# Graph attention on one core: one hold a block for the row gathers, query and key reflected per head, one merged product, and the first gathers spread over the first stage

## The chip, the cores and the metric

The kernel runs on one core of one Trainium2 chip. The core has five engines, each with a queue of its own: TensorE (PE: matrix products and transposes into PSUM; PEld is its weight load), VectorE (DVE), ScalarE (ACT), GpSimd (POOL) and SyncE (SP). [...] The metric is the device time of one execution in microseconds (us). Lower is better.

## The reference

A graph of 12,500 nodes and 212,500 edges, 128 features, eight heads of 16. The edges are sorted by their destination.

```python
h = jnp.maximum(_layernorm(x, axis=-1), 0.0)
q = (h @ Wq.T + bq).reshape(N, 8, 16)
k = (edge_attr @ Wk.T + bk).reshape(-1, 8, 16)
v = (h @ Wv.T + bv).reshape(N, 8, 16)
qs, qd = q[src], q[dst]
in_m   = jnp.sum(qs * k,  axis=-1)
out_m  = jnp.sum(qd * k,  axis=-1)
diag_m = jnp.sum(qs * qd, axis=-1)
score = (_segment_softmax(in_m / 4, dst, N) + _segment_softmax(out_m / 4, dst, N)
         + _segment_softmax(diag_m / 4, dst, N)) * edge_weight ** lam
h = segment_sum(score[..., None] * v[dst], dst)
return x + leaky_relu(h.reshape(N, 128) @ Wo.T + bo, 0.1)
```

Three logits for each edge and head, each a sum over 16 features; for these, only inner products of q and k within a head matter, so any rotation or reflection applied to both within a head leaves them as they are.

## The kernel before

**First stage.** 25 groups of four tiles of 128 nodes. In turn g, from -2 on, ACT rectifies group g+2 (`rectify`, L932), PE turns group g+1 (`turn_h`, L939; ACT copies it to hT, L941) and projects group g to q (`nodes_q`, L947); DVE adds the bias (L950) and SP stores the rows into `q_table` in DRAM. Beside it, DVE takes the statistics of the layer norm (L1064), and `aside(turn)` does other small jobs of that turn.

**Gathers.** For each edge the row of its source node is fetched by an indirect DMA on POOL (`gather`, L706): a block is 512 edges, four gathers of 128 rows of 128 floats. The first `RAW` = 24 blocks fetch rows of x and compute q from them in the loop, so they need not wait for q_table: 15 blocks are issued in turn -2 and 9 in turn 9 of the first stage. Five more blocks, and some single rows, fetch from q_table once it is whole.

**Main loop.** 415 blocks, one an iteration g; five blocks (s = g mod 5) are a turn t. In iteration g

- POOL gathers the rows of block g+26 (`LOOK`), into one of 28 buffers;
- PE turns the edge features of block g+2 (`turn`, tile eT_ps with one buffer, L1247; ACT copies them out, L1249), spreads q to the edges of block g+1 by a one-hot product (`spread_q`, qd_ps, L1264; ACT copies it to qd, L1267) and computes k of block g+1 (`project`: the bias as a product of 3 rows and 512 columns, L1254, then four products with the weights, L1256);
- DVE forms the three products of block g and sums them by head (`logits`, L1275 to L1278);
- ACT makes the one-hot rows of block g+3 (L697, L698).

By s, other steps on a whole turn follow: scans along the edges for the maxima and sums (L1338 to L1390), the exponentials, the selection of the ends of segments (`show_ends`, d_ps L1423, then ACT's L1426 and L1427), and the rows of sums (w_ps L1437, l_ps L1298).

**Order.** `pin` ties each instruction behind the previous one on its engine, so every engine works in the order in which the code is written. A dictionary `behind` holds POOL back: gather j of block g+26 waits, by a semaphore, for a PE instruction of iteration g-1.

```python
if (g - LOOK, j) in behind:
    tc.add_manual_dep(rows.ins, behind[g - LOOK, j], ...Sync..., reason="close behind the products")
```

`behind[g+1, 0]` is the last transpose of `turn(g + 2)`, `[g+1, 1]` the last product of `spread_q(g + 1)`, `[g+1, 2]` that of `project(g + 1)`, and `[g+1, 3]` PE's last instruction of the steps by s.

Of the kernel before, what the change touches and what calls it, by code (L numbers as in the profile page):

```python
# [7 lines left out]
F32 = mybir.dt.float32  # L8
# [8 lines left out]
HEADS = 8  # L17
DIM = 16
# [454 lines left out]
def ordered_path(ctx: ExitStack, tc: tile.TileContext, flag, x, src, dst, edge_attr, edge_weight,  # L473
# [102 lines left out]

    eps = consts.tile([P, 1], F32, name="eps")
# [17 lines left out]
    bv3, bk3, bo3 = [b3[:, i, None, :].to_broadcast([3, JN, F]) for i in range(3)]  # L595
    bq_all = consts.tile([P, F], F32, name="bq_all")
# [105 lines left out]
    def gather(g):  # L702
        if g < end:
            qq = qqs[g] = firsts[g] if g < FIRST else gath.tile([P, JN, F], F32, name="qq")
            for j in range(JN):
                rows = pin(nc.gpsimd.indirect_dma_start(  # L706
                    out=qq[:, j, :], out_offset=None, in_=x if g < RAW else q_table,
                    in_offset=bass.IndirectOffsetOnAxis(
                        ap=sources[g // S][:, g % S, j:j + 1], axis=0)))
# [63 lines left out]
    with tc.tile_pool(name="prep", bufs=1) as prep, \  # L773
# [4 lines left out]
        lam_sb = prep.tile([RW, 1], F32, name="lam_sb")  # L778
        w_in = prep.tile([P, 4, F], F32, name="w_in")
# [24 lines left out]
        pin(nc.sync.dma_start(bq_all, bq[None, :].to_broadcast([P, F])))  # L804
# [10 lines left out]
        def load_b():  # L815
            for i, b in enumerate((bv, bk, bo)):
                pin(nc.sync.dma_start(b_row[:, i, :], b[None, :]))

# [85 lines left out]

        def turn_w(i, to):
# [143 lines left out]
        turn_w(0, wq)  # L1049
# [189 lines left out]
    with tc.tile_pool(name="work", bufs=2) as work, \  # L1239
            tc.tile_pool(name="scan", bufs=2) as scan, \  # L1240
            tc.tile_pool(name="ps", bufs=1, space=PSUM) as ps:
        ks, eTs, qds, q_ps, lTs = {}, {}, {}, {}, {}
# [9 lines left out]
        def project(g):  # L1252
            k_ps = ks[g] = ps.tile([P, JN, F], F32, name="k_ps", bufs=2)
            pin(nc.tensor.matmul(k_ps, ones3, bk3, start=True, stop=False))  # L1254
            for j in range(JN):
                pin(nc.tensor.matmul(k_ps[:, j, :], eTs[g][:, j, :], wk, start=False,  # L1256
                                     stop=(j == JN - 1)))
            del eTs[g]

        def spread_q(g):  # L1260
            s, d = g % S, st[g // S]
            qd_ps = q_ps[g] = ps.tile([P, JN, F], F32, name="qd_ps", bufs=2)
            for j in range(JN):
                pin(nc.tensor.matmul(qd_ps[:, j, :], ohs[g][:, j * P:(j + 1) * P],  # L1264
                                     d["win"][:, s, :], start=(j == 0), stop=(j == JN - 1)))
            qds[g] = work.tile([P, JN, F], F32, name="qd")
            pin(nc.scalar.copy(qds[g], qd_ps))  # L1267
            del ohs[g]

        def logits(g):  # L1270
# [4 lines left out]
            pin(nc.vector.tensor_mul(prod[:, :, 1, :], qqs[g], q_ps[g]))  # L1275
            pin(nc.vector.tensor_mul(prod[:, :, 0, :], qqs[g], ks[g]))  # L1276
            pin(nc.vector.tensor_mul(prod[:, :, 2, :], qds[g], ks[g]))  # L1277
# [3 lines left out]
            del ks[g], qds[g], q_ps[g], qqs[g]  # L1281
# [397 lines left out]
        turn(0)  # L1679
        spread_q(0)  # L1680
        project(0)
        turn(1)
        raw_rectify(SOON)
        for g in range(end):
# [7 lines left out]
            if g + 2 < end:  # L1692
                turn(g + 2)
                behind[g + 1, 0] = pinned[products]
            if g + 1 < end:
                spread_q(g + 1)
# [39 lines left out]
            behind[g + 1, 3] = pinned[products]  # L1736
# [63 lines left out]
        names = ("eT_ps", "k_ps", "qd_ps", "qd_ps", "k_ps")  # L1800
        for r in range(len(rest) + 2):
            if r < len(rest):
                of = rest[r]
                of.score = score[:, r * JN:(r + 1) * JN]
                scores_of(ends_ab[:, r * JN:r * JN + of.n], of.score[:, :of.n])
                of.weigh(of.held)
                of.turn(small([P, JN, P], "node_ps"))
                of.project_o(ps.tile([P, JN, F], F32, name=names[r], bufs=1 if r == 0 else 2))
# [48 lines left out]
```

## Time and profile before

| | |
|---|---|
| median of 3 runs (lowest to highest) | 2730.74 us (2729.23 to 2732.47) |
| the profiled execution: its own time, its span | 2727.95 us, 2726.2 us |
| mean granted clock of TensorE (1 is full) | 0.745 |
| busy: PE, DVE, ACT, POOL | 71%, 76%, 52%, 58% |
| gathers from q_table (L706): count, busy, mean | 1564, 1479.2 us, 946 ns |
| L706, idle before it | 912.7 us, 336.7 of it "issue" |
| first stage / loop with gathers / rest, from the timeline | to about 205 us / to 2543 us / to 2726 us |

A group of instructions reads: line, engine, operation, destination <- sources, shapes, count, then busy time and the mean of one in ns, then the time that the engine stood idle just before them and what ended it. "remote" is a releaser which the profile can't name; "issue" is time in which the engine waited for nothing that is seen. A row of waits gives the engine, its line, the releaser, and after the colon the sum in us, how often, and the longest. A row of the timeline gives the start and the duration in us.

### The profile page before, as it was taken

How to read it: one execution, taken by the hardware profiler on the slowest of the kernel's cores; microseconds unless marked ns; L12 is line 12 of the kernel's file. 1: busy time of each engine (PE TensorE's matmuls, PEld its weight loads, DVE VectorE, ACT ScalarE, POOL GpSimd, SP SyncE). 2: the span in 40 equal slices, each digit the busy share in tenths (PEclk: the TensorE clock that was granted, in tenths of full speed). 3: DMA queues.
4: the chain of work that ended last, by engine and by line, in shares of the span. 5: the costliest groups of instructions: out<-in, count | busy, mean ns of one | idle time of the engine just before them, and what ended most of it. 6: DMA issues, size and time to landing. Idle time of an engine off the chain costs nothing.

```text
span 2726.2 us, 37924 instructions
## 1 busy us (share of the span) xinstructions
PE 1941.1 (71%) x10956; PEld 1524.3 (56%) x10956; DVE 2071.3 (76%) x2887; ACT 1409.7 (52%) x2662; POOL 1585.3 (58%) x1683
## 2 busy tenths in 40 slices
PE   2366776777767777677777777777777776777885
PEld 1245655555555555555555655656556565555664
DVE  2265887777778778778877878877878787787995
ACT  1355864445555555555545555554545555555673
POOL 7516566666666666666666666666666666666200
PEclk9876887776777777777667767766767677776786
DMA  6256444544454454544445444444444544454431
GB/s 177 76 165 175 133 123 126 141 140 127 132 146 132 134 147 140 138 138 125 140 121 137 131 128 132 131 130 123 128 141 112 140 135 121 128 139 129 125 85 52
DMA packets 378950, 355.75 MB, mean 130 GB/s; under 512 B 192898, under 2 KB 298637, under 8 KB 378527
## 3 DMA queue, kind: packets, MB, share of 16 engines
q1 hardware_dynamic: 310109, 238.12, 30.6%
q0 software_dynamic: 53184, 108.92, 15.1%
q10 hardware_dynamic: 15440, 6.20, 0.9%
q8 instruction: 90, 1.47, 0.2%
q14 instruction: 127, 1.04, 0.1%
HBM read 320.83 MB, written 32.17 MB: 129 GB/s over the span
## 4 chain that ended last, share of the span: by engine, by line
PE 44%; DVE 16%; ACT 13%; another core or an unknown queue 12%; issue 11%; DMA 1%; DVEq 1%; POOL 1%; SPq 0%; ACTq 0%; POOLq 0%
PE k_ps L1256 12%; PE w_ps L1437 7%; PE eT_ps L1247 7%; DVE lT L1278 4%; PE qd_ps L1264 4%; PE k_ps L1254 3%; PE node_ps L1186 2%; DVE prod L1276 2%; ACT qd L1267 2%; ACT relb L697 2%; DVE prod L1275 2%; DVE prod L1277 2%; ACT oh L698 2%; PE m_ps L1381 2%
## 5 line engine op out<-in xcount | busy, mean ns | idle before, releaser
L706 POOL DMA_INDIRECT qq<-q_table,sources x1564 | 1479.2, 946 | 912.7 <-issue 336.7
L1278 DVE TENSOR_REDUCE lT<-prod 128x96 f32<-128x1536 f32 x415 | 727.4, 1753 | 14.3
L1256 PE MATMUL k_ps<-wk,eT 128*128 128x128 f32 x3320 | 621.5, 343 | 18.8 <-issue 17.1
L1256 PEld LDWEIGHTS k_ps<-wk,eT 128*128 128x128 f32 x3320 | 524.3, 240 | 171.6 <-issue 170.6
L1247 PE MATMUL eT_ps<-ident,ea 128*128 128x128 f32 x1660 | 346.5, 345 | 206.6 <-issue 129.7
L1276 DVE TENSOR_TENSOR prod<-qq,k_ps 128x512 f32<-128x512 f32 x412 | 280.7, 681 | 203.5 <-remote 166.3
L1247 PEld LDWEIGHTS eT_ps<-ident,ea 128*128 128x128 f32 x1660 | 247.9, 178 | 286.2 <-issue 173.1
L1249 ACT COPY eT<-eT_ps 128x512 f32<-128x512 f32 x415 | 240.7, 580 | 322.8 <-remote 122.6
L1267 ACT COPY qd<-qd_ps 128x512 f32<-128x512 f32 x415 | 244.8, 590 | 313.1 <-PE qd_ps L1264 88.5
L1437 PE MATMUL w_ps<-back,sel 128*126 128x144 f32 (+1 forms) x1296 | 232.1, 356 | 169.0 <-ACT sel L1427 134.4
L1275 DVE TENSOR_TENSOR prod<-qq,qd_ps 128x512 f32<-128x512 f32 x412 | 279.9, 679 | 89.2 <-issue 47.9
L1437 PEld LDWEIGHTS w_ps<-back,sel 128*126 128x126 f32 (+1 forms) x1296 | 218.2, 247 | 183.4 <-ACT sel L1427 144.2
L697 ACT ACTIVATE relb<-relb,before 126x512 bf16<-126x512 bf16 x415 | 303.1, 730 | 0.0
L1277 DVE TENSOR_TENSOR prod<-qd,k_ps 128x512 f32<-128x512 f32 x415 | 281.8, 679 | 0.0
L698 ACT ACTIVATE oh<-relb 126x512 bf16<-126x512 bf16 x415 | 261.3, 630 | 13.2
L1264 PE MATMUL qd_ps<-win,oh 126*128 126x128 bf16 x1660 | 205.6, 258 | 26.6 <-issue 13.7
L1254 PE MATMUL k_ps<-b,ones 3*128 3x512 bf16 x415 | 191.4, 461 | 23.0 <-DVE prod L1277 10.9
L1264 PEld LDWEIGHTS <-oh 126*128 126x128 bf16 x1660 | 164.2, 120 | 48.0 <-issue 34.1
L1381 PE MATMUL m_ps<-ident,m 120*128 120x120 f32 x332 | 76.1, 364 | 107.6 <-issue 59.0
L1426 ACT ACTIVATE sel<-d_ps 128x420 f32<-128x420 f32 x168 | 78.5, 514 | 139.0 <-remote 127.7
L1391 ACT ACTIVATE back<-back 128x480 f32<-128x480 f32 x83 | 50.0, 602 | 142.6 <-DVE back L1390 63.2
L1381 PEld LDWEIGHTS m_ps<-ident,m 120*128 120x128 f32 x332 | 53.1, 215 | 124.5 <-issue 82.6
(234 smaller groups left out, 1934.9 us busy)
## 6 DMA issues: line engine op xcount, KB each, us to landing
ea<-in_edge_attr_dram SPq DMA_DIRECT2D x415, 256.0 KB
relb<-rel_d SPq DMA_DIRECT2D x83, 630.0 KB
qq<-q_table,sources POOLq DMA_INDIRECT x1564
win<-q_table SPq DMA_DIRECT2D x415, 31.5 KB
far<-far_d SPq DMA_DIRECT2D x84, 120.2 KB
q_table<-q SPq DMA_DIRECT2D x24, 384.0 KB
sums<-rows SPq DMA_DIRECT2D x411, 7.9 KB
q_table<-xq SPq DMA_DIRECT2D x24, 256.0 KB
```

The costliest lines, as they stand in the source:

```text
L697: pin(nc.scalar.activation(d, d, AF.Abs, bias=before[:K3]))
L698: pin(nc.scalar.activation(oh, d, AF.Relu, bias=1.0, scale=-1.0))
L706: rows = pin(nc.gpsimd.indirect_dma_start(out=qq[:, j, :], out_offset=None, in_=x if g < RAW else q_table, in_offset=bass.IndirectOffsetOn ...
L1247: pin(nc.tensor.transpose(eT_ps[:, j, :], eas[g][:, j * F:(j + 1) * F], ident))
L1256: pin(nc.tensor.matmul(k_ps[:, j, :], eTs[g][:, j, :], wk, start=False, stop=(j == JN - 1)))
L1264: pin(nc.tensor.matmul(qd_ps[:, j, :], ohs[g][:, j * P:(j + 1) * P], d["win"][:, s, :], start=(j == 0), stop=(j == JN - 1)))
L1267: pin(nc.scalar.copy(qds[g], qd_ps))
L1275: pin(nc.vector.tensor_mul(prod[:, :, 1, :], qqs[g], q_ps[g]))
L1276: pin(nc.vector.tensor_mul(prod[:, :, 0, :], qqs[g], ks[g]))
L1277: pin(nc.vector.tensor_mul(prod[:, :, 2, :], qds[g], ks[g]))
L1278: pin(nc.vector.tensor_reduce(lTs[t][:, :, s, :], prod.rearrange("p j i (h d) -> p j (i h) d", d=DIM), AX.X, ALU.add))
L1437: pin(nc.tensor.matmul(w_ps[:(hi - lo) * W, lo:hi].rearrange("p s c -> p (s c)"), d["sel"][:n, j, lo:hi, :].rearrange("p s w -> p (s w)"), ...
```

## The change

- **One hold a block.** `gather` of block g+26 takes one hold, on its first gather: the last product of `spread_q(g)`. The other three of a block have none.
- **q and k reflected.** Ahead of the first stage a Householder reflection per head is worked out from bk (`bring_to_size`, `reflect`: some twenty small VectorE operations and one root on ACT), which turns bk's 16 elements of a head onto the first. Wq, Wk and bq are reflected with it (the turn of the weights by the identity becomes a product with `axes`). So k's bias has one element a head, and is added by a product of 3 rows and 32 columns, now behind k's four products.
- **Merged product.** q and k of a block lie in one PSUM tile `qk_ps` (two buffers), k is projected ahead of q, and one VectorE product of 1024 elements replaces two of 512.
- **First gathers spread.** Of the 24 raw blocks six are issued in turn -2, the others one a turn in 18 of the turns 0 to 21, each with its first gather held behind the last product of that turn's `nodes_q`.

```diff
-    def gather(g):
+    def gather(g, held=None):
...
-                if (g - LOOK, j) in behind:
-                    tc.add_manual_dep(rows.ins, behind[g - LOOK, j], mybir.DependencyInfo(
+                held = behind.get((g - LOOK, j), held)
+                if held is not None:
+                    tc.add_manual_dep(rows.ins, held, mybir.DependencyInfo(
...
+                held = None
...
+        def bring_to_size():
+            pin(nc.vector.tensor_reduce(top, heads_of(bk_all), AX.X, ALU.max))
...
+            pin(nc.scalar.activation(low, square, AF.Sqrt))
...
+        def reflect():
...
+            pin(nc.vector.tensor_copy(axes, ident))
+            v_both = v[:, None, :].to_broadcast([P, 2, F])
+            pin(nc.vector.tensor_mul(w, turned, v_both))
...
+            pin(nc.vector.tensor_sub(turned, turned, w))
...
         def turn_w(i, to):
-            pin(nc.tensor.transpose(w_ps, w_in[:, i, :], ident))
+            if i in (0, 2):
+                pin(nc.tensor.matmul(w_ps, w_in[:, i, :], axes, start=True, stop=True))
...
-        turn_w(0, wq)
+        bring_to_size()
...
+            if g == -2:
+                reflect()
             if 0 <= g + 1 < GN:
                 turn_h(g + 1)
+            if g == -1:
+                turn_w(0, wq)
             if g >= 0:
                 nodes_q(g)
...
-            if g == -2:
-                for of in range(3 * S):
-                    gather(of)
+            for of in range(RAW):
+                turn = (5 * of - 30) // 4
+                if max(turn, -2) == g:
+                    gather(of, pinned[str(mybir.EngineType.PE)] if g >= 0 else None)
             aside(g)
             if g == 9:
                 fetch_few()
-                for of in range(3 * S, RAW):
-                    gather(of)
...
         def project(g):
-            k_ps = ks[g] = ps.tile([P, JN, F], F32, name="k_ps", bufs=2)
-            pin(nc.tensor.matmul(k_ps, ones3, bk3, start=True, stop=False))
+            qks[g] = ps.tile([P, 2, JN, F], F32, name="qk_ps", bufs=2)
+            k_ps = qks[g][:, 0]
             for j in range(JN):
-                pin(nc.tensor.matmul(k_ps[:, j, :], eTs[g][:, j, :], wk, start=False,
-                                     stop=(j == JN - 1)))
+                pin(nc.tensor.matmul(k_ps[:, j, :], eTs[g][:, j, :], wk, start=(j == 0), stop=False))
+            pin(nc.tensor.matmul(k_ps.rearrange("p j (h d) -> p j h d", d=DIM)[:, :, :, 0], ones3, bk_lead,
+                                 start=False, stop=True))
...
-            pin(nc.vector.tensor_mul(prod[:, :, 1, :], qqs[g], q_ps[g]))
-            pin(nc.vector.tensor_mul(prod[:, :, 0, :], qqs[g], ks[g]))
-            pin(nc.vector.tensor_mul(prod[:, :, 2, :], qds[g], ks[g]))
+            pin(nc.vector.tensor_mul(prod[:, :, 0:2, :].rearrange("p j i f -> p i j f"),
+                                     qqs[g][:, None].to_broadcast([P, 2, JN, F]), qks[g]))
+            pin(nc.vector.tensor_mul(prod[:, :, 2, :], qds[g], qks[g][:, 0]))
...
             if g + 2 < end:
                 turn(g + 2)
-                behind[g + 1, 0] = pinned[products]
             if g + 1 < end:
+                project(g + 1)
                 spread_q(g + 1)
-                behind[g + 1, 1] = pinned[products]
-                project(g + 1)
-                behind[g + 1, 2] = pinned[products]
+                behind[g + 1, 0] = pinned[products]
...
-            behind[g + 1, 3] = pinned[products]
```

On PE, one iteration of the loop before (eT_ps: the turned edge features; oh: one-hot rows; win: the window of q; b and ones: bias and ones; three more pairs of LDWEIGHTS and MATMUL on oh are left out):

```order
L1247 MATMUL eT_ps<-ident,ea 128x128 x4
L1264 LDWEIGHTS oh
L1264 MATMUL qd_ps<-win,oh 128x128
...
L1254 LDWEIGHTS ones_88
L1254 MATMUL k_ps<-b_94,ones_88 128x512
L1256 MATMUL k_ps<-wk,eT 128x128 x4
```

and the same iteration now (the last two rows, too, stand four times):

```order
L1308 MATMUL eT_ps<-ident,ea 128x128 x4
L1317 MATMUL qk_ps<-wk,eT 128x128 x4
L1318 LDWEIGHTS ones_92
L1318 MATMUL qk_ps<-b_98,ones_92 128x32
L1326 LDWEIGHTS oh
L1326 MATMUL qk_ps<-win,oh 128x128
```

k has moved ahead of q, and its bias from in front of the products to behind them, 32 columns wide.

On POOL, gathers in the loop before, with the semaphores that they wait for (PE_49 is PE's, the hold; DVE_49 the buffer; the DMASW ones earlier gathers):

```order
L706 DMA qq<-q_table,sources 128x128 [waits DMASW2_49,DVE_49,PE_49]
L706 DMA qq<-q_table,sources 128x128 [waits DMASW3_49,PE_49]
L706 DMA qq<-q_table,sources 128x128 [waits DMASW4_49,PE_49]
L706 DMA qq<-q_table,sources 128x128 [waits DMASW5_49,PE_49]
L706 DMA qq<-q_table,sources 128x128 [waits DMASW6_49,DVE_49,PE_49]
```

and at the same place now:

```order
L711 DMA qq<-q_table,sources 128x128 [waits DMASW2_49,DVE_49,PE_49]
L711 DMA qq<-q_table,sources 128x128 [waits DMASW3_49]
L711 DMA qq<-q_table,sources 128x128 [waits DMASW4_49]
L711 DMA qq<-q_table,sources 128x128 [waits DMASW5_49]
L711 DMA qq<-q_table,sources 128x128 [waits DMASW6_49,DVE_49,PE_49]
```

PE's semaphore stands at the first gather of a block alone.

On DVE, the logits of a block in the loop before (prod: the products; lT: the logits), and the next block's first two:

```order
L1275 TENSOR_TENSOR prod<-qq,qd_ps 128x4x128 [waits DMASW3_49,DMASW4_49,DMASW2_49,DMASW5_49,DVE_49,Activation_49]
L1276 TENSOR_TENSOR prod<-qq,k_ps 128x4x128 [waits PE_49]
L1277 TENSOR_TENSOR prod<-qd,k_ps 128x4x128
L1278 TENSOR_REDUCE lT<-prod 128x4x24 [waits DVE_49]
L1275 TENSOR_TENSOR prod<-qq,qd_ps 128x4x128 [waits DMASW1_49,DMASW6_49,DMASW0_49,DMASW7_49,DVE_49,Activation_49]
```

and now, with a step of another line between two blocks:

```order
L1337 TENSOR_TENSOR prod<-qq,qk_ps 128x2x4x128 [waits DMASW4_49,DMASW3_49,DMASW5_49,DMASW2_49,Activation_49]
L1339 TENSOR_TENSOR prod<-qd,qk_ps 128x4x128
L1340 TENSOR_REDUCE lT<-prod 128x4x24 [waits DVE_49]
L1431 SCALAR_TENSOR_TENSOR m<-far,head,l_ps 120x512
L1337 TENSOR_TENSOR prod<-qq,qk_ps 128x2x4x128 [waits DMASW1_49,DMASW6_49,DMASW0_49,DMASW7_49,DVE_49,Activation_49]
```

Two products have become one of twice the size, and the wait for PE ahead of the second has gone; the first waits for ACT, whose copy of qd stands behind PE's k and q.

More of the change, by code (lines that the diff above doesn't have):

```diff
@@ L594, in ordered_path @@
     b3 = consts.tile([3, 3, F], BF, name="b3")
-    bv3, bk3, bo3 = [b3[:, i, None, :].to_broadcast([3, JN, F]) for i in range(3)]
-    bq_all = consts.tile([P, F], F32, name="bq_all")
+    bv3, bo3 = [b3[:, i, None, :].to_broadcast([3, JN, F]) for i in (0, 2)]
+    bk_lead = b3[:, 1, None, 0::DIM].to_broadcast([3, JN, HEADS])
     inv = consts.tile([P, NI], F32, name="inv")
@@ L778, in ordered_path @@
         lam_sb = prep.tile([RW, 1], F32, name="lam_sb")
+        room = node.tile([P, JN * 3 * F // 2], F32, name="room", tag="q3", bufs=2)
         w_in = prep.tile([P, 4, F], F32, name="w_in")
@@ L1261, in spread_q @@
             s, d = g % S, st[g // S]
-            qd_ps = q_ps[g] = ps.tile([P, JN, F], F32, name="qd_ps", bufs=2)
+            qd_ps = qks[g][:, 1]
             for j in range(JN):
@@ L1679, in ordered_path @@
         turn(0)
+        project(0)
         spread_q(0)
-        project(0)
         turn(1)
@@ L1693, in ordered_path @@
                 turn(g + 2)
+            if g + 1 < end:
+                project(g + 1)
+                spread_q(g + 1)
                 behind[g + 1, 0] = pinned[products]
[L1695 to L1699 removed]
             logits(g)
@@ L1799, in ordered_path @@
             halves_of(ab, engine)
-        names = ("eT_ps", "k_ps", "qd_ps", "qd_ps", "k_ps")
+        places_o = [ps.tile([P, JN, F], F32, name="eT_ps", bufs=1)]
+        for r in range(2):
+            qk_ps = ps.tile([P, 2, JN, F], F32, name="qk_ps", bufs=2)
+            places_o += [qk_ps[:, 0], qk_ps[:, 1]]
         for r in range(len(rest) + 2):
```

50 lines of the change are left out of this document (45 added, 5 removed).

## The prediction

> **What bounds the kernel now.** I read the page's busy shares first, then its groups, the waits, the timeline of single blocks, and tables by stretch. No engine is full:
>
> ```profile
> PE 1941.1 (71%) x10956; PEld 1524.3 (56%) x10956; DVE 2071.3 (76%) x2887; ACT 1409.7 (52%) x2662; POOL 1585.3 (58%) x1683
> L706 POOL DMA_INDIRECT qq<-q_table,sources x1564 | 1479.2, 946 | 912.7 <-issue 336.7
> L1278 DVE TENSOR_REDUCE lT<-prod 128x96 f32<-128x1536 f32 x415 | 727.4, 1753 | 14.3
> L1276 DVE TENSOR_TENSOR prod<-qq,k_ps 128x512 f32<-128x512 f32 x412 | 280.7, 681 | 203.5 <-remote 166.3
> L1254 PE MATMUL k_ps<-b,ones 3*128 3x512 bf16 x415 | 191.4, 461 | 23.0 <-DVE prod L1277 10.9
> ```
>
> A gather is busy 0.946 us, and its successor follows 0.30 us later, so four gathers, one block, occupy POOL for 4 x 1.25 = 4.99 us. The second product of a block (L1276) waits 203.5 us, most of it for "remote", a releaser that the profile cannot name. The waits name others with the same releaser:
>
> ```profile
> POOL qq L706 <- remote: 224.8, 142, 4.5
> DVE prod L1276 <- remote: 174.9, 81, 8.6
> ACT sel L1426 <- remote: 127.7, 49, 5.2
> ```
>
> The timeline of one such place tells what it is (start, duration, engine, operation, idle before it):
>
> ```profile
> 1292.16 0.94 POOL L706 DMA_INDIRECT qq<-q_table,sources  x1 [1.78 <-remote]
> 1293.76 2.08 PE L1256 MATMUL k_ps<-wk,eT 128*128 128x128 f32 x8
> 1295.77 0.88 PE L1423 MATMUL d_ps<-shows,ends_t 21*128 21x420 bf16 x2
> ...
> 1300.90 0.94 POOL L706 DMA_INDIRECT qq<-q_table,sources  x1 [0.30 <-issue]
> 1303.57 0.69 DVE L1276 TENSOR_TENSOR prod<-qq,k_ps 128x512 f32<-128x512 f32 x1 [3.26 <-remote]
> 1303.60 0.93 ACT L1426 ACTIVATE sel<-d_ps 128x420 f32<-128x420 f32 x2 [5.16 <-remote]
> 1303.80 0.94 POOL L706 DMA_INDIRECT qq<-q_table,sources  x1 [1.95 <-remote]
> ```
>
> PE had written k by 1295.84 and d_ps by 1296.65, yet DVE, ACT and POOL, which wait for PE, all go on within 0.23 us of each other at 1303.6. Between 1292.16 and 1300.90 POOL had issued eight gathers without a pause. I read this so: while gathers follow one another, PE's completions reach nobody, or late; they come in one burst once POOL stands still. I call that a flush. Here the next gather starts 2.90 us after the last one's start; after a run of four it is 2.32:
>
> ```profile
> 1220.16 0.94 POOL L706 DMA_INDIRECT qq<-q_table,sources  x1 [1.77 <-PE eT_ps L1247]
> ...
> 1223.90 0.94 POOL L706 DMA_INDIRECT qq<-q_table,sources  x1 [0.30 <-issue]
> 1226.05 0.35 DVE L1346 TENSOR_TENSOR_SCAN u_head<-far,carry,h_ps 120x64 f32<-120x64 bf16 x1 [1.66 <-remote]
> 1226.10 0.58 ACT L1249 COPY eT<-eT_ps 128x512 f32<-128x512 f32 x1 [1.86 <-remote]
> 1226.22 0.94 POOL L706 DMA_INDIRECT qq<-q_table,sources  x1 [1.38 <-remote]
> ```
>
> So the pace of the loop is the gathers' own time plus flushes. A table by stretch, with L1278 alone (one a block: stretch, length, DVE busy, count, clock), gives it:
>
> ```profile
> 320.00:500.00 180.00, 50.96 (x30) 0.79 0.47 131
> 500.00:2000.00 1500.00, 443.33 (x253) 0.73 0.48 133
> 2000.00:2540.00 540.00, 159.50 (x91) 0.72 0.48 131
> 2560.00:2655.00 95.00, 35.05 (x20) 0.84 0.33 93
> ```
>
> 374 blocks in 2220 us are 5.94 us a block, 0.95 above 4.99; once no gather is left (the last row) a block takes 95/20 = 4.75.
>
> The first stage shows the same thing undisguised. The waits up to 260 us, then L950 (one a group of four node tiles) by stretch, then L706 by stretch:
>
> ```profile
> DVE xq L950 <- remote: 95.2, 5, 31.4
> ACT hT L941 <- remote: 71.1, 4, 30.8
> 0.00:35.00 35.00, 0.69 (x1) 1.00 0.90 255
> 35.00:112.00 77.00, 2.08 (x3) 0.92 0.26 70
> 147.00:204.60 57.60, 10.01 (x15) 0.82 0.59 175
> 0.00:35.00 35.00, 23.05 (x25) 1.00 0.90 255
> 35.00:112.00 77.00, 52.57 (x56) 0.92 0.26 70
> ```
>
> In 112 us POOL issues 81 gathers and the node stage completes 4 of its 25 groups; after 147 us, with no gather, it does 15 in 57.6 us, 3.84 us a group.
>
> **The change part by part.** *First stage.* Now 24 gathers stand ahead of it and 18 blocks are spread over turns 0 to 21, one block a turn, each held behind that turn's nodes_q. The 24 end at 4.6 + 24 x 1.25 = 34.6 us, the flush after them (2.9 us for eight, longer for more) at about 38. In a turn with a block POOL needs 3 x 1.25 + 2.32 = 6.06 us, and a group's work (3.84) fits beside it: the next group's transposes stand ahead of nodes_q on PE, so one flush releases ACT's copy of one group and DVE's addition of the other. 18 x 6.06 + 7 x 3.84 = 136; the stage ends at 38 + 136 = 174 instead of 204.6: -30. Bounds: if every second turn gets its signal without a flush (4.99), 18 x 0.53 = 10 us more; with gathers hidden altogether, -45. If a turn needs two flushes (3.74 + 2 x 2.32 = 8.4), 18 x 2.3 = 42 worse: +12. The reflection puts some twenty small VectorE operations ahead of the first projection; they lie beside the 24 gathers, during which DVE has little to do (one L950 in 35 us), so nothing; uncovered, twenty of at most one L950 each (2.08/3 = 0.69) are under 14 us. The 20 gathers that need the finished q_table, behind the stage, stay.
>
> *One hold a block.* Each gather had its own; now the first waits for q of block g (the last of project and spread_q, one iteration ahead), the other three for nothing of PE's. Queued behind the held gather on POOL are the other three and all later ones; nobody needs them for 26 blocks, so the wait itself delays no one. What counts is how often POOL stands still. A pause at each block costs 2.32 - 1.25 = 1.07 us a block; at every second block (run of eight) (2.90 - 1.25)/2 = 0.83; from 2.32 and 2.90 a pause grows by 0.145 a gather, so at every fourth block (4.06 - 1.25)/4 = 0.70. Before it is 0.95. Four holds can stop a run at any gather, one only at multiples of four, so flushes should become rather fewer, and each comes when PE's k and q for DVE are both there. I take 0.91, between one and two blocks a run: -0.04 x 374 = -15. Bounds: 0.70 gives -93, 1.07 gives +45.
>
> *Bias and merged product.* The 3x512 matmul (0.461 us) becomes one of 3x32. The smallest here, and the cost of a wider reduction per element, are:
>
> ```profile
> L1306 PE MATMUL h_ps<-ident,lT 16*120 16x16 f32 x328 | 33.6, 212 | 10.8 <-ACT rows L1442 5.6 <-issue 4.5 <-ACT hT L1612 0.4
> L1390 DVE TENSOR_TENSOR back<-lT,m_ps 128x480 f32<-128x480 f32 x83 | 53.8, 648 | 59.5 <-PE d_ps L1423 23.7 <-remote 21.5 <-PE qd_ps L1264 9.3
> 2600.81 0.68 DVE L1275 TENSOR_TENSOR prod<-qq,qd_ps 128x512 f32<-128x512 f32 x1
> 2601.41 0.68 DVE L1276 TENSOR_TENSOR prod<-qq,k_ps 128x512 f32<-128x512 f32 x1
> 2602.01 0.68 DVE L1277 TENSOR_TENSOR prod<-qd,k_ps 128x512 f32<-128x512 f32 x1
> 2550.00:2600.00 50.00, 40.31 (x286) 32.59 (x285) 49.13 (x61) 34.09 (x64) 0.00 (x0) 0.90 0.38 113
> ```
>
> By 212 ns PE saves 0.25 us a block. In the loop with gathers a flush comes later than PE, so this is hidden unless PE itself is late at a flush; it is part of my 0.91. 480 elements take 0.648 and 512 take 0.681, 1.03 ns an element; 1024 then take 1.21, and occupy DVE for about 1.13 against two starts 0.60 apart. In the last 26 blocks DVE is the bound (49.13 of 50 us busy): 26 x 0.07 = -2. In the order the merged product waits for ACT's copy of qd, made after PE's k and q; before, the second product waited for PE itself. After a flush that is one ACT copy later (0.58 as in the row at 1226.10), two if eT's stands ahead. What hides it is that DVE has 5.94 - 4.75 = 1.19 us a block to spare, so nothing; with that cover gone in one block of three, 374/3 x 0.58 = +72.
>
> Sum against the profiled execution: 2727.95 (span 2726.2) - 30 - 15 - 2 = 2681. The median of the runs, 2730.74, lies 2.8 above; the forecast for it is 2684.
>
> The Trainium skill's page "DMA: Bandwidth & Descriptors", section "Anatomy of one DMA — SWDGE (gpsimd) path", calls descriptor generation small, with many descriptors emitted before its cost shows. By that the loop would run at 4.75 us, 445 us less; 1564 gathers at 946 ns each say otherwise, and the sum goes by them.
>
> **The rivals.** *Flushes become rare.* k and q reach POOL before a run ends, and it pauses every fourth block. For it: the three unheld gathers, and PE's shorter work. Against it: in the two samples above, signals come when POOL stands still. Pace 5.69: 2684 + 15 - 93 = 2606, or less if signals arrive without any pause.
>
> *A flush at every block, slower than before.* eT_ps has one buffer, so each iteration of PE needs ACT's copy, which needs PE's signal, thus a flush. If PE then finishes only about one block between two flushes, POOL stops at each block: +45 instead of -15. If PE's k and q are moreover still in work when POOL has come to rest, the pause lasts longer; it decides once it is over 1.03 us a block (0.95 + 32/374, which eats up the first stage and the drain). With a pause of 1.15 (1.07, and 0.4 us of PE in one block of five) the time is 2684 + 90 = 2774; with 1.07 it is 2744. I take 2755. For it: PE is 71% busy, and the merged product's later start holds back the buffer that PE's next k needs.
>
> *A colder PE.* The same eight k matmuls took 2.08 us at 1293.76, and in the drain
>
> ```profile
> 2603.04 1.16 PE L1256 MATMUL k_ps<-wk,eT 128*128 128x128 f32 x8
> ```
>
> The granted clock is 0.73 in the loop and 0.84 in the drain. Less PE work and longer common pauses could lower it: at 0.73 the two rates mix to some 1.66 us, so wholly at the low one k takes 0.42 more a block. PE is 44% of the chain below; 374 x 0.42 x 0.44 = +69, 2753.
>
> ```profile
> PE 44%; DVE 16%; ACT 13%; another core or an unknown queue 12%; issue 11%; DMA 1%; DVEq 1%; POOL 1%; SPq 0%; ACTq 0%; POOLq 0%
> ```
>
> The Trainium skill, "TensorE: Matmul & The Clock Gate", section "Part 1: The HAM clock gate (the "warmup" mystery)", says that an idle window of about 3.4 us halves PE's clock: a rule against taking work from PE. The trace bears out both rates.
>
> *The first stage does not shrink.* Two flushes a turn, or its DMAs and VectorE's statistics bind: 2684 + 30 to 42, 2714 to 2726.
>
> **How the numbers follow.** A measurement of this kernel tells 0.2%, 5.5 us, from no change. My forecast has 0.51, rare flushes 0.18, a flush at every block 0.17, a colder PE 0.05, the first stage unchanged 0.09, half of it within 0.2%. That is faster 0.73, same 0.05, slower 0.22. The range goes from 2600, below the rare flushes' price, to 2765, between 2755 and 2774; about 1 in 10 lies beyond each end.
>
> **What would show it.** Right: L950 no longer waits 30 us in one piece, the loop's first L1278 comes 30 us earlier, and POOL's waits hold longer runs than one block. If blocks between 320 and 2500 us take over 6.03 us, the loop's step is wrong; under 5.8, flushes are rare. If the granted clock of the loop falls below 0.68, the colder PE. If the first stage ends after 195 us, its step is wrong.

## The result, and the profile after

| | before | changed |
|---|---|---|
| median of 6 runs (lowest to highest), same chip | 2729.98 us (2725.88 to 2732.47) | 2682.77 us (2672.71 to 2690.16) |
| the profiled execution: its own time, its span | 2727.95, 2726.2 us | 2672.71, 2670.9 us |
| mean granted clock of TensorE | 0.745 | 0.772 |

The ratio is 0.9827, 95% interval 0.9806 to 0.9848: 47 us faster, against a forecast of 2684 us. The profiled execution of the changed kernel was the fastest of its six, so the two spans differ by 55 us and not by 47.

Three groups of the page after (L711 is the gather, L1337 the merged product, L1340 the reduction), and the new bias product from the table by line:

```profile
PE 1738.7 (65%) x10958; PEld 1450.1 (54%) x10958; DVE 2043.9 (77%) x2496; ACT 1395.5 (52%) x2663; POOL 1589.2 (59%) x1683
L711 POOL DMA_INDIRECT qq<-q_table,sources x1564 | 1482.3, 948 | 849.9 <-issue 405.3
L1337 DVE TENSOR_TENSOR prod<-qq,qk_ps 128x1024 f32<-128x1024 f32 x412 | 500.1, 1214 | 192.1 <-ACT qd L1329 157.3
L1318 PE MATMUL qk_ps<-b,ones 3*128 3x32 bf16 x415 | 91.0, 219 | 4.1 <-issue 4.1
```

PE is busy 202 us less: 100 us of that is the bias product (191.4 us before), and most of the rest are the same products, each a little shorter at a higher granted clock (k's four: 343 ns each before, 330 now, at 0.745 and 0.772). Where did the time come from? DVE's addition of q's bias, once a group of the first stage, first of before and then of the changed kernel (least, median and longest in ns, start of the first and the last), and the same line of the changed kernel by stretch:

```profile
L950 DVE TENSOR_TENSOR xq<-q_ps,bq_all x25: 412/691/693, 15.9 to 203.6; 128x512 f32<-128x512 f32 x24, 128x256 f32<-128x256 f32 x1
```

```profile
L1008 DVE TENSOR_TENSOR xq<-q_ps,turned x25: 412/685/693, 21.6 to 154.5; 128x512 f32<-128x512 f32 x24, 128x256 f32<-128x256 f32 x1
0.00:35.00 35.00, 0.69 (x1) 0.81 0.89 251
35.00:112.00 77.00, 8.90 (x13) 0.66 0.45 127
112.00:160.00 48.00, 7.25 (x11) 0.84 0.73 214
```

The stage is over 49 us earlier, and the loop's first reduction starts at 162.8 us instead of 210.1. Between 35 and 112 us, where before 3 groups were done, 13 are. The loop by stretch (L1340, once a block):

```profile
320.00:500.00 180.00, 52.59 (x30) 0.74 0.49 133
500.00:2000.00 1500.00, 443.49 (x253) 0.78 0.48 133
2000.00:2480.00 480.00, 141.99 (x81) 0.77 0.48 130
2490.00:2600.00 110.00, 40.50 (x24) 0.80 0.34 98
```

364 blocks in 2160 us are 5.93 us a block, nearly the pace of before (5.94); in the long middle stretch the two counts are equal, 253. Finer, by the starts of the reductions of blocks 20 to 380, it is 5.92 against 5.95. Of the 55 us between the two spans, 47 lie ahead of the loop's first reduction and 9.6 between that and the last gather (at 2542.9 us before, 2486.0 now); behind it the changed kernel takes 1.6 us more. The loop's 9.6 are about as much as the profiled execution lies under its median, so they can't be told from scatter in this pair. Nearly the whole gain lies in the first stage. In the loop the waits have changed hands: before, DVE's second product and ACT's selection waited for the remote releaser; now it is ACT's two copies, and PE and DVE wait for these.

```profile
PE eT_ps L1308 <- ACT eT L1310: 321.0, 81, 7.8
ACT eT L1310 <- remote: 288.2, 78, 6.8
POOL qq L711 <- remote: 225.8, 108, 4.8
DVE prod L1337 <- ACT qd L1329: 178.5, 87, 17.6
ACT qd L1329 <- remote: 178.4, 63, 13.5
```

One such place in the timeline:

```profile
1292.93 0.94 POOL L711 DMA_INDIRECT qq<-q_table,sources  x1 [2.05 <-remote]
...
1296.08 0.61 PE L1326 MATMUL qk_ps<-win,oh 126*128 126x128 bf16 x4
...
1296.72 0.59 ACT L1329 COPY qd<-qk_ps 128x512 f32<-128x512 f32 x1 [0.88 <-issue]
...
1297.28 1.06 PE L1308 MATMUL eT_ps<-ident,ea 128*128 128x128 f32 x4
...
1300.20 0.65 DVE L1452 TENSOR_TENSOR back<-lT,m_ps 128x480 f32<-128x480 f32 x1 [1.62 <-PE d_ps L1485]
...
1300.89 0.60 ACT L1453 ACTIVATE back<-back 128x480 f32<-128x480 f32 x1 [2.30 <-DVE back L1452]
...
1301.69 0.94 POOL L711 DMA_INDIRECT qq<-q_table,sources  x1 [0.30 <-issue]
...
1304.45 0.59 ACT L1310 COPY eT<-eT_ps 128x512 f32<-128x512 f32 x1 [2.96 <-remote]
1304.83 0.94 POOL L711 DMA_INDIRECT qq<-q_table,sources  x1 [2.19 <-remote]
```

PE had finished eT_ps at 1298.34; ACT copies it at 1304.45, 6.1 us later. POOL starts again 0.38 us after that, 3.14 us after the start of the last of eight gathers. Other rows of this stretch say more. A signal of PE can pass in a row of gathers: PE's L1326 ended at 1296.69, and ACT's copy of its result starts at 1296.72. And DVE's signals are not late: L1452 ended at 1300.85, and ACT's L1453, which waits for it, starts at 1300.89.

The traces keep the times of the engines' signals (semaphore updates), though some records are missing. Each is set here against the latest end of an instruction of the same engine that sends one; the true delay is at least that:

| signals of | trace | stretch, us | recorded | delay: median, longest, us |
|---|---|---|---|---|
| PE | before | 320 to 2000 | 1174 | 1.01, 8.7 |
| PE | changed | 320 to 2000 | 871 | 1.19, 8.5 |
| ACT | changed | 320 to 2000 | 731 | 0.009, 0.010 |
| DVE | changed | 320 to 2000 | 536 | 0.011, 0.012 |
| PE | changed, behind the last gather | 2490 to 2670 | 133 | 0.014, 0.015 |

So of these three engines PE's signals alone are late, in the loop with gathers and not behind it. Of POOL's 186 pauses between the loop's 20th and 380th block, 168 came after a run of eight.

### The profile page after: what moved, and what is told of

The parts are those of the page before. It is cut to its first block, busy times and chain, and to the rows that moved or that the text cites. A ratio compares the mean times of both kernels' runs of the same rounds, so it can differ in the third digit from the quotient of the medians.

```text
span 2670.9 us, 36441 instructions
## 1 busy us (share of the span) xinstructions
PE 1738.7 (65%) x10958; PEld 1450.1 (54%) x10958; DVE 2043.9 (77%) x2496; ACT 1395.5 (52%) x2663; POOL 1589.2 (59%) x1683
## 4 chain that ended last, share of the span: by engine, by line
PE 33%; another core or an unknown queue 20%; ACT 18%; DVE 16%; issue 10%; DVEq 2%; DMA 1%; POOL 1%; ACTq 0%; POOLq 0%; SPq 0%
PE qk_ps L1317 8%; PE eT_ps L1308 7%; PE w_ps L1499 4%; DVE prod L1337 4%; DVE lT L1340 4%; ACT qd L1329 4%; ACT relb L702 3%; PE qk_ps L1326 3%; ACT eT L1310 3%; ACT oh L703 2%; DVE prod L1339 2%; DVEq L1337 2%; PE m_ps L1443 2%; PE node_ps L1247 1%
## 5 line engine op out<-in xcount | busy, mean ns | idle before, releaser
L711 POOL DMA_INDIRECT qq<-q_table,sources x1564 | 1482.3, 948 | 849.9 <-issue 405.3
L1340 DVE TENSOR_REDUCE lT<-prod 128x96 f32<-128x1536 f32 x415 | 727.5, 1753 | 14.4
L1337 DVE TENSOR_TENSOR prod<-qq,qk_ps 128x1024 f32<-128x1024 f32 x412 | 500.1, 1214 | 192.1 <-ACT qd L1329 157.3
L1317 PE MATMUL qk_ps<-wk,eT 128*128 128x128 f32 x3320 | 581.5, 330 | 43.1 <-issue 26.3
L1317 PEld LDWEIGHTS qk_ps<-wk,eT 128*128 128x128 f32 x3320 | 540.2, 245 | 56.9 <-issue 32.9
L1329 ACT COPY qd<-qk_ps 128x512 f32<-128x512 f32 x415 | 244.3, 589 | 459.2 <-remote 178.4
L1339 DVE TENSOR_TENSOR prod<-qd,qk_ps 128x512 f32<-128x512 f32 x415 | 281.9, 679 | 0.0
L1326 PE MATMUL qk_ps<-win,oh 126*128 126x128 bf16 x1660 | 193.8, 247 | 15.9 <-issue 15.6
L1400 DVE TENSOR_TENSOR_SCAN l_ps<-far,carry,l_ps 120x512 f32<-120x512 bf16 x80 | 102.6, 1283 | 108.2 <-remote 68.8
L1326 PEld LDWEIGHTS <-oh 126*128 126x128 bf16 x1660 | 109.5, 107 | 43.0 <-issue 18.7
L1452 DVE TENSOR_TENSOR back<-lT,m_ps 128x480 f32<-128x480 f32 x83 | 54.0, 651 | 77.0 <-remote 33.9
L711 POOL DMA_INDIRECT qq<-in_x_dram,sources x84 | 81.5, 970 | 45.4 <-issue 22.3
L1431 DVE TENSOR_TENSOR_SCAN m<-far,head,l_ps 120x512 f32<-120x512 bf16 x81 | 102.9, 1271 | 0.0
```

Source lines behind the costliest of these rows:

```text
L711: rows = pin(nc.gpsimd.indirect_dma_start(out=qq[:, j, :], out_offset=None, in_=x if g < RAW else q_table, in_offset=bass.IndirectOffsetOn ...
L1337: pin(nc.vector.tensor_mul(prod[:, :, 0:2, :].rearrange("p j i f -> p i j f"), qqs[g][:, None].to_broadcast([P, 2, JN, F]), qks[g]))
L1339: pin(nc.vector.tensor_mul(prod[:, :, 2, :], qds[g], qks[g][:, 0]))
L1340: pin(nc.vector.tensor_reduce(lTs[t][:, :, s, :], prod.rearrange("p j i (h d) -> p j (i h) d", d=DIM), AX.X, ALU.add))
```

## The experiments

Theory: while gathers follow one another, PE's completions (its signals) reach ACT, DVE and POOL late; the first stage suffered most, and spreading its gathers is the gain; the loop's pace is four gathers and a share of a flush, whatever PE and DVE do. Rivals: the shorter work of PE and DVE gives the gain; the holds do.

The runs took place on several chips, and the kernel before shows two kinds of them: 2730, 2760 and 2762 us in three sets of runs (the last two on chips 6 and 5, the first on one without a number), 2176 us each time in three others (chips 8, 3 and 1). I call them the kind with flushes and the quick kind. Each numbered chip appears in one set alone, so it is not shown that the kind stays with the chip. Ratios are always to the kernel before in the same set.

| kernel | before there, us | ratio, 95% interval |
|---|---|---|
| the change | 2729.98 | 0.9827 [0.9806, 0.9848] |
| before, gathers spread | 2759.99 | 0.9808 [0.9778, 0.9838] |
| changed, gathers not spread | 2759.99 | 0.9979 [0.9964, 0.9994] |
| changed, four holds | 2759.99 | 0.9828 [0.9801, 0.9855] |
| before, one hold | 2759.99 | 0.9962 [0.9945, 0.9979] |
| changed, two products | 2761.88 | 0.9802 [0.9786, 0.9819] |
| the change | 2176.22 | 0.9960 [0.9946, 0.9974] |
| before, spread and one hold | 2176.51 | 1.0000 [0.9989, 1.0012] |
| changed, no hold | 2176.51, 2176.22, 2176.21 | 0.9957, 0.9968, 0.9980 |
| changed, hold on each fourth block | 2176.51 | 0.9961 [0.9949, 0.9974] |
| changed, memset behind each gather | 2176.51 | 1.0225 [1.0208, 1.0242] |

**The kernel before with the gathers spread, alone.**

```diff
-            if g == -2:
-                for of in range(3 * S):
-                    gather(of)
+            for of in range(RAW):
+                turn = (5 * of - 30) // 4
+                if max(turn, -2) == g:
+                    gather(of, pinned[str(mybir.EngineType.PE)] if g >= 0 else None)
             if g == 9:
                 fetch_few()
-                for of in range(3 * S, RAW):
-                    gather(of)
```

> The kernel before, with one part of the change alone: the 24 raw blocks spread over the turns of the first stage, one held gather each. Theory (the stage stood still under runs of gathers, and the loop hardly changed): the first reduction of the loop starts near 163 us instead of 210, the loop's pace stays 5.94 us a block, the time is 2730 - 42 = 2688 us, between 2680 and 2698. Rival (the gain is PE's and DVE's shorter work and the single hold): the stage moves by less than 15 us, 2715 to 2730.

2707.59 us against 2759.99 on this chip, 52 us less, where 42 were expected; the absolute figures expected were those of a chip 30 us faster. The first reduction starts at 160.4 us (163 was expected). Its waits up to 210 us and its reductions (L1279) in the loop:

```profile
DVE xq L952 <- remote: 32.9, 3, 25.3
500.00:2000.00 1500.00, 435.52 (x249) 0.73 0.49 131
```

DVE's remote wait in the first stage, 95.2 us before, is a third of that, and the ratio is that of the whole change. The theory holds.

**The changed kernel with the gathers in two lots again** (the same edit the other way round).

> The changed kernel with the raw gathers back in two lots, 60 in turn -2 and 36 in turn 9. Theory: the first reduction of the loop is back near 210 us, and the time is 2683 + 42 = 2725, between 2715 and 2733. Rival (the gain lies in the loop's shorter work): 2683 to 2698.

2754.31 us, 6 us under the kernel before: without the spread little is left. The first reduction is back at 214.3 us. Its reductions (L1341), then its DVE's wait up to 210 us:

```profile
500.00:2000.00 1500.00, 438.27 (x250) 0.77 0.49 132
DVE xq L1008 <- remote: 79.9, 4, 30.3
```

A rival for the stage would be that the gathers' transfers slow the stage's own. What DVE waits for there is PE, though. From the kernel before, in its first row of 60 gathers:

```profile
43.48 0.95 POOL L706 DMA_INDIRECT qq<-in_x_dram,sources  x1 [0.30 <-issue]
43.99 0.69 DVE L950 TENSOR_TENSOR xq<-q_ps,bq_all 128x512 f32<-128x512 f32 x1 [24.37 <-remote]
44.73 0.94 POOL L706 DMA_INDIRECT qq<-in_x_dram,sources  x1 [0.30 <-issue]
```

This is the second group's addition, and PE had ended that group's projection (L947) at 18.07 us, 26 us earlier. It also shows that "late" is the word, and not "never": the signal came in the middle of the row.

**The changed kernel with four holds.**

```diff
                 turn(g + 2)
+                behind[g + 1, 0] = pinned[products]
             if g + 1 < end:
                 project(g + 1)
+                behind[g + 1, 1] = pinned[products]
                 spread_q(g + 1)
-                behind[g + 1, 0] = pinned[products]
+                behind[g + 1, 2] = pinned[products]
...
+            behind[g + 1, 3] = pinned[products]
```

> The changed kernel with a hold on each of the four gathers of a block (behind turn, project, spread_q and the last PE step, as they stood before). Theory: runs of gathers become 5 to 8 long again, three pauses in five blocks, the loop's pace goes from 5.92 to 5.95 at most 6.0 a block: 2683 to 2700 us. Rival (four holds cost the loop dearly, since each can stop POOL): over 2710.

2711.04 us, 49 us under before: 0.9828, where the theory's 2683 to 2700 on the first chip are 0.983 to 0.989 and the rival's 2710 is 0.993. Runs are mixed again (33 pauses after five gathers, 53 after six, 48 after seven, 51 after eight), and the pace is 249 blocks in 1500 us (6.02 us each, blocks 20 to 380), as in the kernel before with its gathers spread and its four holds (249, 6.03). Four holds do not cost the loop dearly.

**The kernel before with one hold.**

```diff
                 turn(g + 2)
-                behind[g + 1, 0] = pinned[products]
             if g + 1 < end:
                 spread_q(g + 1)
-                behind[g + 1, 1] = pinned[products]
                 project(g + 1)
-                behind[g + 1, 2] = pinned[products]
+                behind[g + 1, 0] = pinned[products]
...
-            behind[g + 1, 3] = pinned[products]
```

> The kernel before with one hold a block, on the first gather, behind the last product of k (the same place on PE as in the changed kernel). Theory: runs of eight gathers as in the changed kernel, 3.07 us from the last start of a run to the next, pace 5.90 to 5.95: 2715 to 2732 us. Rival 1 (one hold alone needs the shorter PE work to be kept up with): a flush at every block, 6.06 a block and more, 2765 or more. Rival 2 (the single hold is the whole gain in the loop and more): under 2705.

2748.68 us, 11 us under before, a ratio of 0.9962 (the theory's 2715 to 2732 on the first chip are 0.9945 to 1.0007). It keeps up with one hold at 250 blocks in 1500 us (6.00 us each, blocks 20 to 380), without the shorter PE work; 156 of its 202 pauses follow eight gathers. One hold gains the loop little, some 0.4%. Against the changed kernel unspread (2754.31) it differs only by the reflection, the short bias, the merged product and the order of k and q: together these are worth nothing on this chip. The 6 us that they seem to cost are within the two intervals; in the traces they lie ahead of the loop (first reduction at 205.8 us here, at 214.3 there), while a block of the loop takes 6.00 us here and 5.99 there.

**The kernel before with both, spread and one hold** (the two edits above).

> The kernel before with two parts of the change, the spread raw gathers and one hold a block (behind the last product of k), without the reflection, the wide product and the new order of k and q. Theory (the parts add up: 52 us and 11 us were measured for them alone, and the rest of the change is worth nothing or less): 63 us under the kernel before of the same chip, between 53 and 70, faster than the whole change. Rival (the reflection and the merged product carry part of the gain): 35 to 48 us under it.

This kernel ran on a chip on which the kernel before takes 2176.51 us, and took 2177.84: neither the theory's 63 us nor the rival's. The waits of POOL show why:

```profile
POOL qq L706 <- issue: 389.5, 1278, 0.3
POOL ends_ab L1796 <- DMA qq<-sums: 49.2, 1, 49.2
POOL qq L706 <- DMA qq<-q_table,sources: 18.9, 62, 0.3
```

No engine's wait for the remote releaser is among the sixty largest, and no pause longer than 1.75 us lies in the loop between the 20th and the 380th block. PE's signals are recorded within 0.015 us of its work, all 1554 between 320 and 2000 us. There are no flushes here to be saved. Whether the sum of parts holds where there are flushes was not measured.

**The changed kernel without holds, and with a hold on every fourth block.**

```diff
-                behind[g + 1, 0] = pinned[products]
```

```diff
-                behind[g + 1, 0] = pinned[products]
+                if g % 4 == 0:
+                    behind[g + 1, 0] = pinned[products]
```

> The changed kernel with no hold on the gathers in the loop; POOL is stopped only by the buffers, which DVE gives back. Theory (DVE and ACT hear nothing of PE while gathers follow one another, and POOL is then stopped by a buffer, that is by a starved DVE, and not by its own pause): a pause lasts the flush of about 3 us and DVE's two products (1.9 us) more, 5 us for eight gathers, 6.9 us a block, 350 us slower than the changed kernel. Rival (the holds only cost): pace between 5.0 and 5.7, 80 us or more faster.

> The changed kernel with a hold on every fourth block alone. Theory: with runs of sixteen the last start of a run would stand 4.06 us before the next, 5.69 us a block; but only two blocks' buffers are spare, so DVE, starved, stops POOL before that: 6.2 to 6.9 us a block, 100 to 350 us slower than the changed kernel. Rival (rare flushes): 5.6 to 5.75, 65 us or more faster.

The kernel without holds ran twice more:

> The changed kernel without holds in the loop, again, in case this chip shows flushes. Then theory (DVE and ACT hear nothing of PE while gathers follow one another, so POOL is stopped by a buffer that a starved DVE gives back late): 6.2 to 7.1 us a block, 100 us or more slower than the changed kernel. Rival (holds only cost): 80 us or more faster. Without flushes: within 5 us of the changed kernel, since DVE then sets the pace and POOL's buffers stop it anyway.

> The changed kernel without holds in the loop, beside the kernel before, in case this chip shows flushes (the kernel before at 2700 us or more; the changed kernel had 0.9827 of it). Theory (DVE and ACT hear nothing of PE while gathers follow one another; without a hold POOL stops only for a buffer that a starved DVE gives back late): 6.2 to 7.1 us a block, a ratio of 1.02 or more. Rival 1 (holds only cost): under 0.955. Rival 2 (the buffers stop POOL as well as the hold does, at the same places): 0.975 to 0.99. Without flushes: 0.995 to 0.998 as twice before.

All four ran on chips of the quick kind: 2167.75, 2168.41, 2169.94 and 2171.89 us, the time of the changed kernel with its holds (2166.88, below). There the holds do nothing. What they do where there are flushes is open: no kernel without them ran on such a chip.

**The changed kernel with a pause behind each gather.**

```diff
                 held = None
+                if g >= AHEAD:
+                    pin(nc.gpsimd.memset(rest_a_while, 0.0))
```

> The changed kernel with a small memset (128 x 64) on POOL behind each gather of the loop, which does nothing else: gathers then follow at some 1.40 to 1.50 us instead of 1.25. Theory A (each gather leaves 0.145 us of work behind that piles up while they follow at 1.25 us, and signals pass once nothing is piled up): no flushes are needed, waits for a remote releaser vanish, 5.6 to 5.9 us a block, 10 to 90 us faster than the changed kernel. Theory B (any run of gathers starves the signals, and only a stop lets them by): runs of eight with pauses as before, (7 x 1.45 + 3)/2 = 6.6 us a block, 250 us slower.

2225.51 us, on a quick chip, so theories A and B were not put to the test. It measured something else. Its gathers by stretch, and the memset from the table by line:

```profile
1000.00:2157.00 1157.00, 856.41 (x896) 0.80 0.57 151
L723 POOL MEMSET rest_a_while<- 128x64 f32 x1544 | 259.8, 168 | 0.9
```

896 gathers in 1157 us are 1.291 us each (1.40 to 1.50 were expected). The last comes at 2156 us; the kernel ends 72 us later.

**The change once more.**

> The changed kernel once more, unaltered, beside the kernel without holds. Where the chip shows flushes (the kernel before at 2700 us or more): ratio 0.980 to 0.985 as in the first result, loop 5.9 us a block. Where it shows none (the kernel before near 2180 us, as where the kernel without holds took 0.9957 of it): theory (the gain is that of flushes in the first stage, which are absent there): ratio 0.994 to 1.000, the loop at 4.7 us a block, bound by DVE; rival (the merged product and the shorter matmul pay once DVE and PE are the bound): under 0.990.

2166.88 us, a ratio of 0.9960, as the theory had it. Theory and rival expected DVE to set the pace, and that is not quite so. Gathers of this run, then reductions (L1340), by stretch:

```profile
1000.00:2096.00 1096.00, 829.83 (x874) 0.80 0.60 159
2096.00:2164.20 68.20, 0.25 (x1) 0.65 0.18 53
1000.00:2096.00 1096.00, 406.71 (x232) 0.80 0.60 159
2096.00:2164.20 68.20, 3.51 (x2) 0.65 0.18 53
```

POOL issues 874 gathers in 1096 us, 1.254 each, 5.02 a block, without a pause, while 232 blocks take DVE only 4.72 each (4.69 by the starts of blocks 20 to 380): DVE eats up the 26 blocks of lead, and two blocks are left when the last gather is out. On such a chip the time is POOL's uninterrupted row of 1662 gathers, 1662 x 1.254 = 2084 us, and some 70 to 80 us behind it. With the memset the pitch is 0.037 us longer, which over 1544 gathers makes 57 us (measured 59). Shorter products touch only what lies behind the last gather: there, in the two traces, the kernel before with spread and one hold, at 4.72 us a block, still needs 84 us, and this one 69, which covers the 0.4% (9 us). And completions pass: from the same timeline,

```profile
1003.50 0.95 POOL L711 DMA_INDIRECT qq<-q_table,sources  x1 [0.30 <-issue]
...
1003.77 0.61 PE L1326 MATMUL qk_ps<-win,oh 126*128 126x128 bf16 x4
...
1004.42 0.58 ACT L1329 COPY qd<-qk_ps 128x512 f32<-128x512 f32 x1 [4.48 <-PE qk_ps L1326]
...
1004.75 0.94 POOL L711 DMA_INDIRECT qq<-q_table,sources  x1 [0.30 <-issue]
```

ACT starts 0.04 us after PE's end, in the middle of a row of gathers at the same 1.25 us. All 1203 recorded signals of PE between 320 and 2000 us come within 0.015 us.

**The changed kernel with the merged product cut in two.**

```diff
-            pin(nc.vector.tensor_mul(prod[:, :, 0:2, :].rearrange("p j i f -> p i j f"),
-                                     qqs[g][:, None].to_broadcast([P, 2, JN, F]), qks[g]))
+            pin(nc.vector.tensor_mul(prod[:, :, 1, :], qqs[g], qks[g][:, 1]))
+            pin(nc.vector.tensor_mul(prod[:, :, 0, :], qqs[g], qks[g][:, 0]))
```

> The changed kernel with its merged product cut in two again (q with q, then q with k, each 512 elements). Where the chip shows no flushes (the kernel before near 2176 us, the changed kernel at 0.996 of it, DVE busy 94% and its loop at 4.69 us a block against 4.72 with the three products of before): theory (DVE sets the pace and the merged product's 0.04 to 0.07 us a block is the whole of that gain): ratio 0.999 to 1.003, 4.72 us a block or more; rival (the gain is PE's shorter bias product and the new order of k and q): 0.995 to 0.998. Where it shows flushes: 0.978 to 0.988, as the changed kernel, since DVE has time to spare there.

2707.74 us against 2761.88, 0.9802, on a chip with flushes, within the 0.978 to 0.988 expected: the merged product is worth nothing that can be seen there (the whole change has 0.9827, on another chip). No version was found that is clearly faster than the changed kernel on both kinds of chip; on those with flushes the kernel before with spread gathers alone is as fast.

## Why the prediction was right, and where it was not

The total was right, 2684 against 2683, and that it was right to 1 us is luck. In the two profiles the first stage gained 47 to 49 us and not 30, the loop 9.6 and not 15, and the drain lost 1.6 instead of gaining 2: 55 us against a forecast of 47. The medians are 47 apart, since the profiled execution of the changed kernel was the fastest of its six.

- **First stage: -30 forecast, -49 measured in the profiles, past the bound of -45.** The mechanism was right, late signals behind rows of gathers; the size was not. The mis-sized term is the "7 x 3.84" in "18 x 6.06 + 7 x 3.84 = 136", 27 us for the turns without a block. From 47.80 to 145.24 us POOL issued 16 blocks, 6.09 us each, which is the forecast's 6.06 (though by fewer and longer pauses than 18 of 2.32 us: the stage's 96 gathers went out in ten runs, of 4, 8 and 12 behind a first one of 28). But DVE finished 20 groups in the same 97 us: the turns without a block cost nothing beside them. Part of this was lost again at the start. The first run was of 28 gathers and not of 24, began at 8.08 us and not at 4.6, and the next gather came at 47.80, where the forecast has the flush over at about 38. The end of that first run, and the first gather of the last run:

```profile
42.09 0.94 POOL L711 DMA_INDIRECT qq<-in_x_dram,sources  x1 [0.30 <-issue]
47.56 0.69 DVE L1008 TENSOR_TENSOR xq<-q_ps,turned 128x512 f32<-128x512 f32 x1 [20.14 <-remote]
47.70 0.59 ACT L999 COPY hT<-h_ps 128x512 f32<-128x512 f32 x1 [15.51 <-remote]
47.80 0.94 POOL L711 DMA_INDIRECT qq<-in_x_dram,sources  x1 [4.77 <-remote]
...
145.24 0.95 POOL L711 DMA_INDIRECT qq<-in_x_dram,sources  x1 [1.42 <-DMA ea<-in_edge_attr_dram]
```

  From 42.09 to 47.80 are 5.71 us from start to start. By the prediction's 0.145 us a gather, 2.32 + 24 x 0.145 = 5.80 was to be expected for 28 gathers, well beyond the two samples that it was drawn from.
- **Loop: -15 forecast, -9.6 measured in the profiles.** Longer runs came as forecast, at every second block mostly, with slightly longer pauses: 3.04 us after eight gathers in the middle of the cases and not 2.90, (3.04 - 1.25)/2 = 0.90 us a block. On chip 6 the kernel before takes 6.00 us a block with one hold, and 6.03 with four and its gathers spread. The shorter bias product, 0.46 to 0.22 us, was hidden behind flushes, as the prediction had it: there a block takes 5.99 us with it and 6.00 without, both with one hold.
- **The reflection,** put at nothing, was not quite: in each trace of the changed kernel that was set beside one without it, the first gather starts 3 to 4 us later (8.08 us against 4.63 in the first pair). It waits for the load of its indices; why that comes later is not shown.
- **Merged product:** 1.21 us was forecast and 1.214 measured. In the drain it gave nothing to be seen: 26 blocks are left behind the last gather both times, at 4.75 us each before and 4.77 now. That it now waits for ACT shows in the waits (178.5 us); that this costs nothing, since the pace is POOL's, is argued and not shown apart.
- **A flush at every block:** did not happen; one iteration of PE for each flush was not the rule. Nor did flushes become rare (5.92 us a block, not 5.69), and the first stage did shrink.
- **A colder PE:** the opposite. With PE at 65% instead of 71% the clock in the middle stretch is 0.78 and not 0.73. It is not the lesser work alone: on chip 6 the changed kernel stands at 0.77 there with one hold a block (gathers not spread) and at 0.73 with four. The Trainium skill's rule ("TensorE: Matmul & The Clock Gate", "Part 1: The HAM clock gate (the "warmup" mystery)") is about single idle windows of some 3.4 us; this trace does not show that less work brings more of them.
- **Descriptors:** by the rule of "DMA: Bandwidth & Descriptors" (the Trainium skill, "Anatomy of one DMA — SWDGE (gpsimd) path"), many descriptors can be emitted before their cost shows. It does not give the time of these gathers, on the quick chips either: there their 1.25 us each are nearly the whole time. How much of that is the making of descriptors no run shows.
- **A count:** "81 gathers" in 112 us takes one gather twice, which lies across 35 us; it is 80.

Not settled: why completions are late on one kind of chip and not on the other, and whether POOL's issuing holds them back or the transfers that it starts. The gathers' pitch is the same, 1.25 us, on both; only the delay differs. The traces of the kind with flushes also hold far fewer records of signals, those of transfers included: 15,883 against 58,730 for the changed kernel. Whether that has the same cause no run shows. The prediction was drawn from a trace of the first kind; on the second the change is worth 0.4%.

## What to carry to other kernels

Where several engines start again within 0.2 us of each other, look for what they have in common, here PE's completions and a row of gathers that had just stopped; then break up the row where others wait for it, before shortening their work. Work taken from engines that wait (100 us of PE's bias product) bought nothing that could be seen here. Where nothing is late, count the gathers: their number times their pitch was nearly the time, and a busy share of 94% on DVE alone pointed at the wrong engine.

## What the runs showed of the hardware that was not expected

The same kernel takes 2730 to 2762 us in three sets of runs and 2176 us in three others, 20% less, at the same pitch of gathers. On the kind with flushes PE's signals, and of the three engines looked at (PE, ACT, DVE) PE's alone, came up to 8.7 us late in the loop with gathers, and 26 us late in a row of 60. Some passed within a row, the others came in a burst once POOL paused. From the start of a row's last gather to the next gather it took 2.3 us after four, 3.04 after eight, 3.5 after twelve and 5.7 after 28. Behind the last gather the same trace shows them within 0.015 us, and so does the quick kind in the middle of a row.
